# A decoder layer in one kernel: router counts spread over more passes, turned tiles in another bank, transposes and W1 products in another place

## The chip, the core and the metric

The kernel runs on one core of a Trainium2 chip. The metric is the device time of one execution in microseconds (us); lower is better. Before the change the median of three runs is 849.79 us (848.02 to 852.45). The profile is one further execution with its own time. Engines: PE is TensorE (matmuls; PEld its weight loads), DVE is VectorE, ACT is ScalarE, POOL is GpSimd, SP issues DMAs.

## What is computed

A decoder layer in float32 on x of 2 batches, 1024 tokens, 256 channels, with a context of 77 tokens for each batch:

```python
x = layernorm(x + causal_self_attention_with_rope(x))        # 16 heads of 64
x = layernorm(x + cross_attention(x, ctx))                   # 16 heads, 77 keys
weights = x @ w_r + b_r                                      # router: one number for each token
threshold = top_k(weights, 512)[-1]                          # per batch
selected = weights > threshold
block = gelu(x @ W1 + b1) @ W2 + b2                          # 256 -> 1024 -> 256
x = layernorm(x + where(selected, block, x))
```

## The kernel before

The tokens of both batches form 16 tiles of 128. The self-attention fills the first 584 us and is left alone by the change. Behind it comes `Prepare` (584 to 617 us): it folds the keys with the query weights (`wqk`) and the values with the output weights; the folded values are stored to DRAM by SP (`vo_d`, L727) and loaded back in another layout (`packed`, L728 and L729), per batch.

**Cross-attention, tile by tile.** `Tile_.turn` (L896) transposes the tile's x on TensorE into a bank of PSUM, and ACT copies it out as `x1T`. `scores` (L903) multiplies it with `wqk`; VectorE takes the maxima (L918) and subtracts them (L920), ACT takes exponentials, `weights` (L926) sums them on VectorE (L929, L931) and scales `e` on GpSimd (L932). `transposes` (L934) turns `e` in ten blocks on TensorE (L942), four to a bank, so in three groups with two blocks in the last; ACT copies them out as `pT`. `output` (L949) multiplies with `packed` (L954); VectorE adds x (y, L956) and starts the layer norm. Its `close` runs later: GpSimd's power (`rs`, L127), VectorE's scaling (x, L128) and the router's dot product (`weigh`, L761), which gives one number in `route`.

**The ring.** The banks that `turn`, `transposes`, `output`, `spread`, `slots`, and the feed-forward's `layer` write come from one pool of four (`ring`), handed out in the order in which the program asks. A bank may be written again when the engine that reads it has done so.

**The router.** A token is taken if fewer than 512 of its batch have a router value at least as large, so each tile's values are compared with all 1024. `spread(first, last)` (L765) transposes the values of tiles first to last so that every partition holds them in a row, and ACT copies the row to `every` (L772). `reach(i, first, last)` (L774) counts on VectorE, for the 128 tokens of tile i, how many values of tiles first to last reach theirs (L777). `select` (L783) makes a 0/1 mask and sums over tiles; `slots` (L789) sums over partitions with two matmuls (L792, L793) and gives each row a place; `scatter` (L805) writes each tile's rows to those places in DRAM with one indirect DMA of GpSimd for a tile (L807); `load` (L813) reads the two halves back as `kept[0]` (taken) and `kept[1]` (SP, L819) once all eight scatters have landed.

**Feed-forward.** `turn` (L838) transposes `kept[0]` (L843); `hidden(f0)` (L846) makes two of the eight W1 blocks, eight matmuls (L852), with gelu on ACT; `layer(j)` (L859) multiplies with W2 (L863), adds b2 (L868), puts x in where fewer than 512 were taken (L869), adds x (L870) and norms; `skipped(j)` (L882) handles the other half. GpSimd writes the rows out (L833).

**What sets the order.** From L978 on, TensorE, VectorE and ACT run in the order in which the program is written; the order on GpSimd and SP is left to the framework's scheduler. The loop (L1019) has passes s = 0 to 16. A pass holds, in this order: the scores and weights of tile s + 1, `output` of tile s - 1, what `midway` has for s, `turn` of tile s + 2, `transposes` of tile s, the `close` of tile s - 1, and what `at_end` has for s. So tile 7, the last of batch 0, is closed in pass 8. Batch 0's counts come in passes 7 to 10, its slots in 11, its scatters in 11 and 12, its load in 13; in pass 15 its rows are turned and batch 1's first six tiles are spread, and after that pass's `close` come `hidden(0)` of batch 0 and six counts of batch 1. Behind the loop come `hidden(2)`, the last two tiles' spread and counts of batch 1, `hidden(4)`, `hidden(6)`, batch 1's slots and scatters, W2 of batch 0 (`late`), batch 1's load and turning, and its feed-forward.

Of the kernel before, what the change touches and what calls it, by code (L numbers as in the profile page):

```python
# [34 lines left out]
def decoder_layer(  # L35
# [117 lines left out]
    with (  # L153
# [74 lines left out]
        class Pair:  # L228
# [151 lines left out]
            def output(self, n):  # L380
                if n == 0:
                    self.po = [ring.tile([P, NT, R32], F32, tag="t", name="po_self") for _ in range(4)]
                for k in range(4):
                    for j in range(2):
                        first = (NT * n + n, NT * (n + 1) + n)[j]
                        step = (1, NT)[j]
                        last = first + (NT - 1 - n) * step + 1

                        for r in range(k if n == NT - 1 else 0, 4):
                            rows = slice(r * R32, (r + 1) * R32)  # L390
                            TE.matmul(  # L391
                                self.po[r][j * D : (j + 1) * D, n:, :],
                                self.v4[rows, 4 * n + k, j * D : (j + 1) * D],
                                p_t[rows, first:last:step, k * R32 : (k + 1) * R32],
                                start=(n == 0 and k == 0), stop=(n == NT - 1 and k == r),
                            )
# [349 lines left out]
    class Router:  # L746
# [15 lines left out]
                dead, self.x2[:, i, :C], w_r, 1.0, b_r, ALU.mult, ALU.add, self.route[:, i : i + 1]  # L762
            )

        def spread(self, first, last):  # L765

            for m in range(first, last, 4):
                e = min(m + 4, last)
                pt = ring.tile([P, 4, P], F32, tag="t", name="pt_r")
                for i in range(m, e):  # L770
                    TE.transpose(pt[:, i - m, :], self.route[:, i : i + 1].to_broadcast([P, P]), ident)
                A.copy(self.every[:, m * P : e * P], pt[:, : e - m, :].rearrange("p i n -> p (i n)"))  # L772

        def reach(self, i, first, last):  # L774

# [37 lines left out]
        def load(self):  # L813
# [3 lines left out]
            for h in range(2):  # L817
# [5 lines left out]
                    tc.add_manual_dep(ins.ins, of.name, sync, reason="all rows are there")  # L823
                self.kept.append(t)

        def numbers(self):
            for t in self.kept:
                r = fp.tile([P, NK2], U32, tag="rows", name="rows", bufs=4)
                V.tensor_copy(r, t[:, :, C])
                self.rows.append(r)  # L830
# [28 lines left out]
        def layer(self, j):  # L859

            po = ring.tile([P, C], F32, tag="t", name="po_ffn")
            for f in range(NF):
                TE.matmul(  # L863
                    po, self.h_t[:, f, j * P : (j + 1) * P], w2[:, f, :], start=(f == 0), stop=(f == NF - 1)
                )
            x2 = self.kept[0][:, j, :C]
            y = fp.tile([P, C], F32, tag="yf", name="y", bufs=5)
            V.tensor_tensor(y, po, b2, ALU.add)  # L868
            V.copy_predicated(y, self.left[:, j : j + 1].to_broadcast([P, C]), x2)  # L869
            V.tensor_tensor(y, y, x2, ALU.add)  # L870
            return self.finish(0, j, y)

        def finish(self, h, j, y):
# [15 lines left out]
    class Tile_:  # L889
# [4 lines left out]
            self.x1 = x1s[b][:, i, :C]  # L894

        def turn(self):  # L896
            self.x_t = c2.tile([P, NC, P], F32, tag="x1T", name="x1T")
            pt = ring.tile([P, NC, P], F32, tag="t", name="pt_x")
            for c in range(NC):
                TE.transpose(pt[:, c, :], self.x1[:, c * P : (c + 1) * P], ident)  # L900
            A.copy(self.x_t, pt)  # L901
# [29 lines left out]
            V.reciprocal(inv, sums)  # L931
            G.tensor_tensor(e, e, inv.unsqueeze(2).to_broadcast([P, HH, S]), ALU.mult)  # L932

        def transposes(self):  # L934
            self.p_t = c2.tile([P, NK, P], F32, tag="pT2", name="pT2")
            e = self.e.rearrange("p h s -> p (h s)")
            for m in range(0, NK, 4):
                n = min(4, NK - m)
                pt = ring.tile([P, 4, P], F32, tag="t", name="pt_p2")
                for k in range(m, m + n):  # L940
                    w = min(P, HS - k * P)
                    TE.transpose(pt[:w, k - m, :], e[:, k * P : k * P + w], ident)  # L942
                whole = n if (m + n) * P <= HS else n - 1
                A.copy(self.p_t[:, m : m + whole, :], pt[:, :whole, :])
                if whole < n:
                    w = HS - (m + whole) * P
                    A.copy(self.p_t[:w, m + whole, :], pt[:w, whole, :])

        def output(self):  # L949

            po = ring.tile([P, C], F32, tag="t", name="po_cross")
            for k in range(NK):
                w = min(P, HS - k * P)
                TE.matmul(po, self.p_t[:w, k, :], packed[self.b][:w, k, :], start=(k == 0), stop=(k == NK - 1))  # L954
            y = work.tile([P, C], F32, tag="y", name="y", bufs=6)
            V.tensor_tensor(y, po, self.x1, ALU.add)  # L956
            last = layernorm(self.x1, y)

            def close():
                last()  # L960
                routers[self.b].weigh(self.i)

            return close

    tiles = [Tile_(b, i) for b in range(B) for i in range(NT)]
    L = NT - 2

    def reaches(r, tiles_, first, last):
        for i in tiles_:
            r.reach(i, first, last)  # L970

    def reached(r):

        reaches(r, range(L), L, NT)
        reaches(r, range(L, NT), 0, NT)
        r.select()

    with tc.manual_schedule(engines={TE.engine, V.engine, A.engine}):  # L978
        first = Prepare()
        k_t = first.context("k")  # L980
        first.turn()
        tiles[0].turn()
        tiles[1].turn()
        first.fold_keys(k_t)
        v_t = first.context("v")
        first.fold_values(v_t, 0)
        first.fold_values(v_t, 1, 0, NP // 2)
        for hh in range(2):
# [12 lines left out]
        wpool = pool("weights", 1)  # L1001
        w1 = load_wide(L0_ffn_W1, "wk")
        w2 = load_tall(L0_ffn_W2)
        routers = [Router(b) for b in range(B)]
        r0, r1 = routers


        midway = {
            L + 1: lambda: r0.spread(0, L), NT + 1: lambda: r0.spread(L, NT), NT + 3: r0.slots,
            NT + L + 1: lambda: (r0.turn(), r1.spread(0, L)),  # L1010
        }
        at_end = {
            NT - 1: lambda: reaches(r0, range(0, 3), 0, L), NT: lambda: reaches(r0, range(3, L), 0, L),
            NT + 1: lambda: reaches(r0, range(L), L, NT),
            NT + 2: lambda: (reaches(r0, range(L, NT), 0, NT), r0.select()),
            NT + 3: lambda: r0.scatter(0, 4), NT + 4: lambda: r0.scatter(4, NT), NT + 5: r0.load,
            NT + 6: r0.numbers, NT + 7: lambda: (r0.hidden(0), reaches(r1, range(L), 0, L)),
        }
        for s in range(B * NT + 1):  # L1019
            if 1 < s + 1 < B * NT:  # L1020
                for hh in range(2):
                    tiles[s + 1].scores(hh)
                for hh in range(2):
                    tiles[s + 1].weights(hh)
            close = tiles[s - 1].output() if s > 0 else None
            midway.get(s, lambda: None)()
            if s + 2 < B * NT:
                tiles[s + 2].turn()
            if s < B * NT:
                tiles[s].transposes()  # L1030
            if close:
                close()
            at_end.get(s, lambda: None)()

        r0.hidden(2)
        r1.spread(L, NT)
        reached(r1)
        r0.hidden(4)
        r0.hidden(6)
        r1.slots()  # L1040
        r1.scatter(0, NT)
        late = [r0.layer(j) for j in range(NK2)]
        r1.load()
        r1.turn()
        for f in late:
            f()
        for f in [r0.skipped(j) for j in range(NK2)]:
            f()
        r1.numbers()
        for f0 in range(0, NF, 2):  # L1050
            r1.hidden(f0)
        for f in [r1.skipped(j) for j in range(NK2)]:
            f()
        for j in range(NK2):
            r1.layer(j)()
# [39 lines left out]
```

## Time and profile before

| | us |
|---|---|
| median of three runs | 849.79 (848.02 to 852.45) |
| the profiled execution's own time | 851.71 |
| its span, first to last instruction | 849.9 |
| busy: TensorE, VectorE, ACT, GpSimd | 791.4, 572.0, 357.4, 364.1 |
| mean granted clock of TensorE | 0.982 of full |
| loop, first scores in it to its last output | 620.4 to 778.3 |
| batch 0's slot product | 729.30 |
| batch 0's scatters on GpSimd | 734.08 to 744.15 |
| batch 1's slot product | 789.70 |
| batch 1's scatters on GpSimd | 791.64 to 801.58 |
| last W2 product's end | 841.6 |

A row of the waits names who waited, for whom, and the total, the number and the longest of these waits. A timeline row gives start and length in us, engine, line, operation, output and inputs, and in brackets the idle time ahead of it with what ended it. A windows row gives, after the stretch and its length, busy time and number of instructions of PE, PEld, DVE, ACT and POOL, then the granted clock (1.00 is full speed), the DMA engines' mean busy share and GB/s. Times are read off one profiled execution.

### The profile page before, as it was taken

What the parts mean: (1) busy time and instruction counts of PE and PEld (TensorE: products, weight loads), DVE (VectorE), ACT (ScalarE), POOL (GpSimd) and SP (SyncE); (2) the same over time, 40 slices, a digit from 0 to 9 for tenths busy, and PEclk for the clock granted to TensorE, in tenths of its full rate; (3) what the DMA queues carried; (4) which work ended last, traced back from release to release, by engine and by line L of the source; (5) the groups of instructions that cost most, each with busy time, mean ns of one, the idle gap of its engine ahead of it and who ended that gap; (6) DMA issues with size and microseconds to landing.
All of it is one profiled execution on the core that took longest, in us unless ns stands there. A gap on an engine that the chain in (4) does not pass through costs nothing.

```text
span 849.9 us, 26576 instructions
## 1 busy us (share of the span) xinstructions
PE 791.4 (93%) x11428; PEld 627.2 (74%) x11428; DVE 572.0 (67%) x1306; ACT 357.4 (42%) x845; POOL 364.1 (43%) x261
## 2 busy tenths in 40 slices
PE   7979999999999999899999988789999999999886
PEld 4547788878778778678788776678778887776645
DVE  2566679767858757578668677444577788866654
ACT  2545556555555556365454554101433333223020
POOL 1732654563573564274372740212023322440473
PEclk9989999999999999999999999999999999999989
DMA  4564596596677669566485377572270000110130
GB/s 160 155 156 99 134 231 148 150 246 163 164 170 189 143 178 237 155 196 168 134 236 116 115 187 187 142 252 82 81 257 1 1 1 1 42 59 1 52 122 25
DMA packets 75040, 113.38 MB, mean 133 GB/s; under 512 B 7249, under 2 KB 61483, under 8 KB 72875
## 3 DMA queue, kind: packets, MB, share of 16 engines
q1 hardware_dynamic: 70315, 73.92, 29.0%
q10 hardware_dynamic: 3072, 33.56, 18.2%
q0 software_dynamic: 1536, 4.20, 1.3%
q8 instruction: 90, 1.47, 0.7%
q14 instruction: 27, 0.22, 0.1%
HBM read 71.77 MB, written 23.11 MB: 112 GB/s over the span
## 4 chain that ended last, share of the span: by engine, by line
PE 79%; DVE 10%; DMA 4%; issue 4%; POOL 2%; ACT 1%; SPq 0%; POOLq 0%; ACTq 0%; DVEq 0%
PE po_self L391 16%; PE ps_scores L323 16%; PE pp_kq L250 13%; PE pp_v L285 6%; PE ps_cross L911 6%; PE po_cross L954 6%; PE po_proj L452 5%; PE po_ffn L863 3%; PE pp_h L852 3%; DVE pT L353 2%; DVE reach L777 2%; DMA v_d<-v 1%; DVE p L336 1%; PE pt_p L942 1%; DVE e L920 1%
## 5 line engine op out<-in xcount | busy, mean ns | idle before, releaser
L344 ACT ACTIVATE p<-p,neg 128x768 f32<-128x768 f32 (+7 forms) x256 | 196.2, 768 | 172.9 <-DVE neg L336 168.9
L336 DVE CUSTOM_DVE_ANT_0 p<-ps_scores,fence 128x512 f32<-128x512 f32 (+7 forms) x256 | 179.4, 750 | 130.2 <-PE ps_scores L323 130.0
L353 DVE STREAM_TRANSPOSE pT<-p 128x768 f32<-128x768 f32 (+7 forms) x256 | 175.6, 740 | 4.7 <-PE po_self L391 3.4
L391 PE MATMUL po_self<-pT,v 32*64 32x256 f32 (+6 forms) x7808 | 160.4, 298 | 19.1 <-issue 14.8
L391 PEld LDWEIGHTS po_self<-pT,v 32*64 32x64 f32 x7808 | 137.5, 132 | 46.1 <-issue 33.8
L323 PE MATMUL ps_scores<-kq 64*128 64x256 f32 (+3 forms) x1064 | 153.2, 419 | 5.5 <-POOL kq L277 5.0
L323 PEld LDWEIGHTS ps_scores<-kq 64*128 64x128 f32 x1064 | 94.9, 190 | 49.3 <-issue 29.3
L270 POOL TENSOR_TENSOR kq<-raw,cos 128x1024 f32<-128x1024 f32 x31 | 73.2, 2362 | 130.6 <-ACT raw L258 130.6
L250 PE MATMUL pp_kq<-xT,w_pair 128*128 128x256 f32 (+2 forms) x528 | 121.8, 384 | 4.0 <-DVE inv L365 2.1
L250 PEld LDWEIGHTS pp_kq<-xT,w_pair 128*128 128x128 f32 x528 | 90.2, 192 | 27.9 <-issue 11.6
L273 POOL TENSOR_TENSOR turned<-turned,sin 128x1024 f32<-128x1024 f32 x31 | 73.2, 2361 | 56.5 <-DMA turned<-raw 50.2
L127 POOL TENSOR_TENSOR rs<-ve,neg_half 128x1 f32<-128x1 f32 x48 | 27.3, 575 | 154.2 <-DVE ve L125 151.1
L932 POOL TENSOR_TENSOR e<-e,inv 128x616 f32<-128x616 f32 x32 | 38.3, 1218 | 116.6 <-DVE inv L931 55.7
L277 POOL TENSOR_TENSOR kq<-kq,turned 128x1024 f32<-128x1024 f32 x31 | 73.5, 2372 | 1.4
L954 PE MATMUL po_cross<-packed,pT 128*128 128x256 f32 (+1 forms) x320 | 71.8, 379 | 0.1
L911 PE MATMUL ps_cross<-wqk,x1T 128*128 128x308 f32 x256 | 69.3, 424 | 1.4 <-ACT x1T L901 1.4
L954 PEld LDWEIGHTS po_cross<-packed,pT 128*128 128x128 f32 (+1 forms) x320 | 60.8, 190 | 10.2 <-issue 0.5
L285 PEld LDWEIGHTS pp_v<-w_pair,xT 128*128 128x128 f32 x512 | 61.1, 192 | 3.2 <-issue 1.5
L285 PE MATMUL pp_v<-w_pair,xT 128*128 128x128 f32 x512 | 62.2, 275 | 0.0
L911 PEld LDWEIGHTS ps_cross<-wqk,x1T 128*128 128x128 f32 x256 | 47.4, 190 | 17.9 <-ACT x1T L901 1.7
L452 PE MATMUL po_proj<-wo,attnT 128*128 128x256 f32 x240 | 56.5, 389 | 3.3 <-DMA attnT<-attn_d 3.3
L924 ACT ACTIVATE e<-e 128x616 f32<-128x616 f32 x32 | 22.9, 717 | 79.2 <-DVE e L920 79.2
(121 smaller groups left out, 795.6 us busy)
## 6 DMA issues: line engine op xcount, KB each, us to landing
v<-v_d ACTq DMA_DIRECT2D x64, 512.0 KB, 7.7
turned<-raw SPq DMA_DIRECT2D x64, 256.0 KB, 5.0
v_d<-v SPq DMA_DIRECT2D x64, 128.0 KB, 4.3
over<-inv_d SPq DMA_DIRECT2D x32, 256.0 KB, 4.2
attn_d<-out_pair SPq DMA_DIRECT2D x15, 512.0 KB, 8.6
attnT<-attn_d SPq DMA_DIRECT2D x8, 512.0 KB, 5.3
attnT<-attn_d SPq DMA_DIRECT2D x3, 896.0 KB, 5.1
vo_d<-vo SPq DMA_DIRECT2D x2, 1232.0 KB
```

The source lines that it names most:

```text
L250: TE.matmul(pp[:, cols], self.w[:, c, "kq".index(of), :], x_ts[self.b, n][:, c, cols], start=(c == 0), stop=(c == NC - 1),)
L270: E.tensor_tensor(self.kq[:, :, n * NB : (n + 1) * NB], self.raw[n], self.twice(cos, n), ALU.mult)
L277: E.tensor_tensor(dst, dst, self.turned[n], ALU.add)
L285: TE.matmul(pv[:, i, :], x_ts[self.b, 2 * n // NT][:, c, toks], self.w[:, c, 2, :], start=(c == 0), stop=(c == NC - 1),)
L323: TE.matmul(self.ps[j][:, cols], self.kq[rows, 1, t * P : (t + 1) * P], self.kq[rows, 0, cols.start - at : cols.stop - at], start=True, st ...
L336: V.tensor_tensor_reduce(p[:, span], self.ps[j][:, span], fence[:, T - (t + 1) * P :], -SCALE, -MASKED, ALU.add, ALU.min, neg[:, i : i + 1],)
L344: A.activation(p[:, span], p[:, span], AF.Exp, bias=neg[:, i : i + 1], scale=-1.0, accum_out=self.sums[:, j, t : t + 1],)
L353: V.transpose(p_t[:, first : first + t * step + 1 : step, :], self.p[g, j][:, span].rearrange("p (n k) -> p n k", k=P),)
L391: TE.matmul(self.po[r][j * D : (j + 1) * D, n:, :], self.v4[rows, 4 * n + k, j * D : (j + 1) * D], p_t[rows, first:last:step, k * R32 : (k ...
L452: TE.matmul(self.po, of, wo[:, c, :], start=(c == 0), stop=(c == NP - 1))
L911: TE.matmul(ps[:, g, : Q * S], self.x_t[:, c, :], wqk[:, c, self.b, h : h + Q, :].rearrange("p h s -> p (h s)"), start=(c == 0), stop=(c = ...
L954: TE.matmul(po, self.p_t[:w, k, :], packed[self.b][:w, k, :], start=(k == 0), stop=(k == NK - 1))
```

## The change

It does six things. (1) `turn` of tile 2 moves ahead of the loop, and `turn` of tile s + 3 is done inside `transposes` of tile s, in the two free quarters of its last bank; its copy by ACT comes after that bank's other copies, and `x1T` gets three buffers. (2) Batch 0's counts are split finer and begin in pass 5 with four tiles' values (passes 5 to 10), scatters are written two to a pass in passes 11 to 14, and batch 1's counts begin in pass 13. (3) The loop ends with pass 14; the last tile's transposes come ahead of the output of the tile before it, and batch 1's seventh value row is spread in the middle of the last output. (4) `hidden(0)` of batch 0 moves behind the last output, the last value row is copied by VectorE, and `hidden(4)` and `hidden(6)` come after batch 1's slots. (5) `ready` adds b2 to `kept[0]` and doubles `kept[0]` ahead of time, so that `layer` has one addition fewer. (6) In the built program the scheduler's order changes on SP: the loads of W1 and W2 (L95, L101) now stand ahead of vo's store and packed's load instead of behind them. The order on GpSimd is the same as before, with all eight scatters of a batch together.

The core of the diff:

```diff
-        def spread(self, first, last):
+        def spread(self, first, last, copy=A.copy):
...
+        def ready(self):
+            x2 = self.kept[0][:, :, :C]
+            self.plus = fp.tile([P, NK2, C], F32, tag="plus", name="plus")
+            V.tensor_tensor(self.plus, x2, b2.unsqueeze(1).to_broadcast([P, NK2, C]), ALU.add)
+            self.double = fp.tile([P, NK2, C], F32, tag="double", name="double")
+            V.tensor_tensor(self.double, x2, x2, ALU.add)
...
-            V.tensor_tensor(y, po, b2, ALU.add)
-            V.copy_predicated(y, self.left[:, j : j + 1].to_broadcast([P, C]), x2)
-            V.tensor_tensor(y, y, x2, ALU.add)
+            V.tensor_tensor(y, po, self.plus[:, j, :], ALU.add)
+            V.copy_predicated(y, self.left[:, j : j + 1].to_broadcast([P, C]), self.double[:, j, :])
...
-            self.x_t = c2.tile([P, NC, P], F32, tag="x1T", name="x1T")
+            self.x_t = c2.tile([P, NC, P], F32, tag="x1T", name="x1T", bufs=3)
...
-        def transposes(self):
+        def transposes(self, ahead=None):
...
+                if ahead and m + n == NK:
+                    ahead.x_t = c2.tile([P, NC, P], F32, tag="x1T", name="x1T", bufs=3)
+                    for c in range(NC):
+                        TE.transpose(pt[:, n + c, :], ahead.x1[:, c * P : (c + 1) * P], ident)
                 A.copy(self.p_t[:, m : m + whole, :], pt[:, :whole, :])
...
+                if ahead and m + n == NK:
+                    A.copy(ahead.x_t, pt[:, n : n + NC, :])
...
-        def output(self):
+        def output(self, midst=None):
...
+                if midst and k == NK // 2:
+                    midst()
...
+        tiles[2].turn()
...
-            L + 1: lambda: r0.spread(0, L), NT + 1: lambda: r0.spread(L, NT), NT + 3: r0.slots,
-            NT + L + 1: lambda: (r0.turn(), r1.spread(0, L)),
+            5: lambda: r0.spread(0, 4), 7: lambda: r0.spread(4, 6), 9: lambda: r0.spread(6, NT), 11: r0.slots,
+            13: lambda: r1.spread(0, 4), NT + 7: lambda: r1.spread(4, 6),
...
-            NT - 1: lambda: reaches(r0, range(0, 3), 0, L), NT: lambda: reaches(r0, range(3, L), 0, L),
-            NT + 1: lambda: reaches(r0, range(L), L, NT),
-            NT + 2: lambda: (reaches(r0, range(L, NT), 0, NT), r0.select()),
-            NT + 3: lambda: r0.scatter(0, 4), NT + 4: lambda: r0.scatter(4, NT), NT + 5: r0.load,
-            NT + 6: r0.numbers, NT + 7: lambda: (r0.hidden(0), reaches(r1, range(L), 0, L)),
+            5: lambda: reaches(r0, (0, 1), 0, 4), 6: lambda: reaches(r0, (2, 3), 0, 4),
+            7: lambda: reaches(r0, range(4), 4, 6), 8: lambda: reaches(r0, (4, 5), 0, 6),
+            9: lambda: reaches(r0, range(6), 6, NT), 10: lambda: (reaches(r0, (6, 7), 0, NT), r0.select()),
+            11: lambda: r0.scatter(0, 2), 12: lambda: r0.scatter(2, 4),
+            13: lambda: (r0.scatter(4, 6), reaches(r1, (0, 1), 0, 4)),
+            14: lambda: (r0.scatter(6, NT), reaches(r1, (2, 3), 0, 4)),
...
-        for s in range(B * NT + 1):
+        for s in range(B * NT - 1):
...
-            if s + 2 < B * NT:
-                tiles[s + 2].turn()
-            if s < B * NT:
-                tiles[s].transposes()
+            tiles[s].transposes(tiles[s + 3] if s + 3 < B * NT else None)
...
+        r0.load()
+        tiles[-1].transposes()
+        close = tiles[-2].output()
+        midway[NT + 7]()
+        r0.turn()
+        close()
+        reaches(r1, range(4), 4, 6)
+        reaches(r1, (4, 5), 0, 6)
+        close = tiles[-1].output(lambda: r1.spread(6, 7))
+        reaches(r1, range(6), 6, 7)
+        r1.reach(6, 0, 7)
+        close()
+        r0.hidden(0)
+        r1.spread(7, NT, V.tensor_copy)
+        reaches(r1, range(7), 7, NT)
+        r1.reach(7, 0, NT)
+        r1.select()
         r0.hidden(2)
-        r1.spread(L, NT)
-        reached(r1)
+        r1.slots()
+        r1.scatter(0, NT)
+        r0.numbers()
+        r0.ready()
         r0.hidden(4)
         r0.hidden(6)
-        r1.slots()
-        r1.scatter(0, NT)
         late = [r0.layer(j) for j in range(NK2)]
...
         r1.numbers()
+        r1.ready()
```

More of the change, by code (lines that the diff above doesn't have):

```diff
@@ L771, in spread @@
                     TE.transpose(pt[:, i - m, :], self.route[:, i : i + 1].to_broadcast([P, P]), ident)
-                A.copy(self.every[:, m * P : e * P], pt[:, : e - m, :].rearrange("p i n -> p (i n)"))
+                copy(self.every[:, m * P : e * P], pt[:, : e - m, :].rearrange("p i n -> p (i n)"))
         def reach(self, i, first, last):
@@ L865, in layer @@
                 )
-            x2 = self.kept[0][:, j, :C]
             y = fp.tile([P, C], F32, tag="yf", name="y", bufs=5)
-            V.tensor_tensor(y, po, b2, ALU.add)
-            V.copy_predicated(y, self.left[:, j : j + 1].to_broadcast([P, C]), x2)
-            V.tensor_tensor(y, y, x2, ALU.add)
+            V.tensor_tensor(y, po, self.plus[:, j, :], ALU.add)
+            V.copy_predicated(y, self.left[:, j : j + 1].to_broadcast([P, C]), self.double[:, j, :])
             return self.finish(0, j, y)
@@ L965, in decoder_layer @@
     tiles = [Tile_(b, i) for b in range(B) for i in range(NT)]
-    L = NT - 2
     def reaches(r, tiles_, first, last):
@@ L970, in reaches @@
             r.reach(i, first, last)
[L972 to L976, printed above, removed]
     with tc.manual_schedule(engines={TE.engine, V.engine, A.engine}):
@@ L1008, in decoder_layer @@
         midway = {
-            L + 1: lambda: r0.spread(0, L), NT + 1: lambda: r0.spread(L, NT), NT + 3: r0.slots,
-            NT + L + 1: lambda: (r0.turn(), r1.spread(0, L)),
+            5: lambda: r0.spread(0, 4), 7: lambda: r0.spread(4, 6), 9: lambda: r0.spread(6, NT), 11: r0.slots,
+            13: lambda: r1.spread(0, 4), NT + 7: lambda: r1.spread(4, 6),
         }
         at_end = {
-            NT - 1: lambda: reaches(r0, range(0, 3), 0, L), NT: lambda: reaches(r0, range(3, L), 0, L),
-            NT + 1: lambda: reaches(r0, range(L), L, NT),
-            NT + 2: lambda: (reaches(r0, range(L, NT), 0, NT), r0.select()),
-            NT + 3: lambda: r0.scatter(0, 4), NT + 4: lambda: r0.scatter(4, NT), NT + 5: r0.load,
-            NT + 6: r0.numbers, NT + 7: lambda: (r0.hidden(0), reaches(r1, range(L), 0, L)),
-        }
-        for s in range(B * NT + 1):
-            if 1 < s + 1 < B * NT:
+            5: lambda: reaches(r0, (0, 1), 0, 4), 6: lambda: reaches(r0, (2, 3), 0, 4),
[4 more added lines that the diff above has]
+            14: lambda: (r0.scatter(6, NT), reaches(r1, (2, 3), 0, 4)),
+        }
+        for s in range(B * NT - 1):
+            if s > 0:
                 for hh in range(2):
```

## Prediction

> **What bounds the kernel now.** I read the page first, then TensorE's waits in the part that the change can touch, then the timelines of TensorE, VectorE and GpSimd there. The built program of the changed kernel holds the same instructions in the same order up to 590 us, so only the last 260 us count.
>
> ```profile
> PE 791.4 (93%) x11428; PEld 627.2 (74%) x11428; DVE 572.0 (67%) x1306; ACT 357.4 (42%) x845; POOL 364.1 (43%) x261
> ...
> PE 79%; DVE 10%; DMA 4%; issue 4%; POOL 2%; ACT 1%; SPq 0%; POOLq 0%; ACTq 0%; DVEq 0%
> ```
>
> TensorE carries the end, and the edit removes no matmul. So it can only win TensorE's waits, and the half clock that follows a long one. Who waited for whom on TensorE, 615 to 850 us (total, times, longest):
>
> ```profile
> PE pt_x L843 <- DMA kept<-comp: 5.4, 1, 5.4
> PE pt_p L942 <- DVE y L956: 3.8, 4, 1.4
> PE ps_cross L911 <- ACT x1T L901: 1.4, 1, 1.4
> PE pp_slot L792 <- DVE sums L787: 0.7, 1, 0.7
> PE pp_h L852 <- ACT x2T L844: 0.5, 1, 0.5
> ```
>
> That is 11.8 us. TensorE's timeline shows where, and what the longest wait does to the work behind it:
>
> ```profile
> 729.92 0.60 PE L942 MATMUL pt_p<-ident,e 128*128 128x128 f32 x4
> 731.93 0.84 PE L942 MATMUL pt_p<-ident,e 128*128 128x128 f32 x6 [1.41 <-DVE y L956]
> ...
> 753.34 0.44 PE L942 MATMUL pt_p<-ident,e 128*128 128x128 f32 x2 [1.23 <-DVE y L956]
> ...
> 809.60 1.94 PE L843 MATMUL pt_x<-ident,kept 128*128 128x128 f32 x8 [5.40 <-DMA kept<-comp]
> 812.00 15.80 PE L852 MATMUL pp_h<-x2T,w_wk 128*128 128x512 f32 x32 [0.46 <-ACT x2T L844]
> ```
>
> The eight transposes of batch 0 take 0.95 (767.84 to 768.79); here 1.96. Thirty-two W1 products at 3.44 per eight (the first of batch 0) are 13.8; here 15.80. So 3.0 us are lost to a clock that the windows show at half:
>
> ```profile
> 804.00:808.00 4.00, 0.20 (x1) 0.00 (x0) 3.59 (x12) 0.00 (x0) 1.21 (x2) 1.00 0.25 53
> 808.00:816.00 8.00, 5.94 (x13) 3.32 (x14) 5.92 (x21) 1.49 (x4) 6.79 (x9) 0.57 0.49 156
> ```
>
> **Part 1, the start.** Tile 2's turning moves ahead of the loop. In pass 0 its transposes stand directly ahead of tile 2's scores, which wait for ACT's copy: 1.4. Afterwards the same two transposes (0.22) stand at 591 us and scores follow without that copy. The extra ACT copy (0.37) falls among copies that wait for VectorE there. **Minus 1.4.**
>
> SP's order changes as well: both FFN weights (1 MB each) now stand ahead of the store of vo and the load of packed. They wait for the last w_v product (601.5), so they do not hold SP (vo's store issues at 606.05), but they share the DMA engines with it. At some 380 GB/s (367, 420 and 347 in 628 to 634) their 2.1 MB take 5.5 us; started at 602.6 they leave 1.2 us of data when the store's first bytes move (606.9). packed lands at 619.4 now, 620.6 then; the first output needs it at 623.0. Cover 2.4, so I cost it at nothing. The other bound: the store waits until both have landed, 10.7 after their issue as now, and starts 6.5 later; that is rival 2.
>
> **Part 2, the loop.** A pass is 9.78 us of TensorE (640.10 to 649.88). A ring of four banks is allotted in order. A pass now takes five (output, turned tile, three of weights), so the third group of weights reuses the bank of its own output and waits for y. With the turned tile in the last bank a pass takes four, and the conflict is left only in passes with counts or slots: 5, 7, 9, 11, 13.
>
> How late is y? When VectorE is behind, it takes 8.07 from the first maximum to the end of the router's dot product (693.51 to 701.58; 1.03 of it waits for GpSimd's rs), y starts at 4.92, and TensorE resumes 0.52 after that start. When it keeps up, the dot product ends 11.49 after the pass's start (690.71 - 679.22). Counts come on top, by their spacing: 0.46 each at 256 wide, 0.934 at 768, 1.20 at 1024; I work out 0.67 at 512 and 1.07 at 896. 128 wide has no row: its columns alone are 0.13, the 256-wide row is 0.46; a line through it with the columns' slope gives 0.33, which I take. Lag of the first maximum behind the pass's start, worked forward (next lag = lag + 8.07 + counts - pass): for before it gives 3.77, 4.86, 4.7, 5.7 in passes 8 to 11, as the trace has it. Step lengths less work give before's true losses: 0.98 + 0.55 + 1.63 + 1.44 = 4.6.
>
> After: counts of 1.34, 1.34, 1.85, 1.87, 2.77, 3.2 (with the selection) in passes 5 to 10 instead of 2.8, 2.8, 2.8, 3.2 in 7 to 10. Lags 2.6, 3.1, 3.3, 3.6, 4.5, 5.9 in passes 6 to 11. In 5, 7 and 9 y is still on time (8.67), so no wait. In pass 11 y starts at 10.87, TensorE resumes at 11.39 and wanted 9.72: 1.7 lost, as before.
>
> Pass 13 hangs on GpSimd:
>
> ```profile
> 733.12 0.55 POOL L127 TENSOR_TENSOR rs<-ve,neg_half 128x1 f32<-128x1 f32 x1
> 734.08 1.20 POOL L807 DMA_INDIRECT comp<-x,slot  x1 [0.42 <-DVE slot L803]
> ...
> 743.19 0.96 POOL L807 DMA_INDIRECT comp<-x,slot  x1 [0.30 <-issue]
> 744.18 2.39 POOL L932 TENSOR_TENSOR e<-e,inv 128x616 f32<-128x616 f32 x2
> 746.53 0.57 POOL L127 TENSOR_TENSOR rs<-ve,neg_half 128x1 f32<-128x1 f32 x1
> ```
>
> Eight scatters (10.1 us) stand ahead of e and rs, and VectorE waits 4.6 for rs. The edit writes two scatters a pass, but GpSimd's queue is not ordered by hand: the built program still has all eight together ahead of tile 13's e. So this part does not do what it says. VectorE is again 5.9 late in pass 13, which now holds four counts' transposes: 1.5 lost. Loop: 4.6 becomes 3.2, **minus 1.4**. Were the scatters in written order, batch 0's rows would come in pass 15 instead of 13; they are not.
>
> **Part 3, the last transposes.** They now follow tile 14's at once. Their second half needs e from GpSimd, 6.67 after the first maximum, which lags 3.8 there: 10.5, wanted 10.0. **Plus 0.6**; a 0.2 wait between transposes and output goes. Batch 0's rows land near pass 13's middle, so their turning does not wait.
>
> **Part 4, behind the loop.** Here the end is set by batch 1's chain: last output, norm, counts, slots, eight scatters, load. From the slot product to the rows' landing it was 19.8 (789.70 to 809.47), the scatters 10.0 of it. Behind the slots stood only W2 (13.9): hence 5.4. Now hidden(4) and hidden(6) stand there too: 0.5 + 6.9 + 13.9 = 21.3, so the 5.4 and its 3.0 of half clock go, with 1.5 to spare.
>
> What is late next: more of the chain must now be crossed with less to do. From output 14's end VectorE has 0.2 + 1.27 (y to ve) + 0.6 (rs) + 0.95 (x, dot), four counts at 256 and two at 768 (3.7), y of tile 15 (1.27), then, queued ahead of x of tile 15, six counts at 128 and one at 896 (3.1), x and dot 0.95: 12.0. TensorE has count transposes and turning 1.35, output 15 with one more 4.43, hidden(0) 3.44: 9.2. It stops 2.8 to 2.9 at spread(7). After that: copy on VectorE 0.5, seven at 128 and one at 1024 (3.6), selection 0.8 = 4.9 against hidden(2) 3.55: 1.4 to 1.5 more.
>
> Does a gap of 2.9 throttle? The row first: after this stop the windows of half a microsecond show the clock at 0.50 from 515.5 to 518.5.
>
> ```profile
> 514.47 1.47 PE L391 MATMUL po_self<-pT,v 32*64 32x128 f32 x73 [2.53 <-issue]
> ```
>
> The Trainium skill (TensorE: Matmul & The Clock Gate, "Part 1: The HAM clock gate") has the clock halved only after a whole idle window of about 3.4 us; by it 2.9 costs nothing. By the row it costs 1.7 (3.4 us at half), but on hidden(2), which ends ahead of the 1.5 wait for slots and is covered by it. I take the row, 0.3 uncovered; bounds 0 and 1.7.
>
> The sums plus and double (two of 128x1024, by 799 ns for 616 wide some 1.3 each) fall on VectorE while TensorE runs hidden(4): nothing; without that cover 2.6. At the end one 0.45 addition after the last W2 product goes: **minus 0.45**. Tail: 0.9 + 5.4 + 3.0 = 9.3 becomes 2.9 + 1.5 + 0.3 + 0.1 = 4.8, **minus 4.5**.
>
> **Sum.** -1.4 -1.4 +0.6 -0.2 -4.5 -0.45 = -7.35. The profiled execution took 851.71 (span 849.9 and 1.8 around it), 1.9 above the median of 849.79: it goes to 844.4, the median to 842.4.
>
> **Rivals.** (1) Narrow counts cost what 256 does (thirteen of them, +0.13 each: 1.7) and the half clock after the gap is uncovered (1.7): 845.8. For it: 256 wide is already above its slope. (2) Weights ahead of vo: packed 6.5 later, the first output stops 2.9, half clock 1.7: 847.0. Against it: the DMA engines stood idle from 600 to 606, so the weights have a start. (3) Slower: the gap at spread(7) starts a half clock that does not end, because hidden(2) and the slots' wait keep TensorE idle by turns. It costs half of the time it lasts; it decides from 23.3 us at half on, which the 24.7 us of work up to batch 0's last W2 product could fill; at 25 us it gives 854.9. Against it: the longest stretch here is 6.8 (808.8 to 815.7). (4) Better: passes 11 and 13 lose nothing: 839.2.
>
> **Chances.** Forecast (840 to 845) 0.62; (4) 0.12; (1) 0.14; (2) 0.08; (3) 0.04. A measurement tells 0.5% (4.2 us) from no change: faster 0.74, same 0.22, slower 0.04. Range 838.5 to 847: (4) without its lower edge, (1) and (2).
>
> **What would show it.** No wait of pt_x for kept in batch 1, and W1 at 13.8 there; a new stop of nearly 3 us at the last count's transpose and one near 1.5 at the slots; in the loop, waits of pt_p for y in passes 11 and 13 alone; eight scatters together. I am wrong if batch 1's rows still come late (slots over 1.5 us later), if VectorE's lag at tile 15 is larger, or if the first output waits for packed.

## The result and the profile after

| | before | after |
|---|---|---|
| median of seven runs (us) | 851.85 (848.02 to 855.7) | 844.62 (843.15 to 849.51) |
| profiled execution: its own time | 851.71 | 849.51 |
| its span | 849.9 | 847.7 |
| from Prepare's first product to batch 0's slot product | 145.02 | 142.07 |
| to batch 1's slot product | 205.42 | 199.53 |
| to the turning of batch 1's rows | 225.32 | 220.73 |
| to the end of the last W2 product | 257.34 | 250.28 |
| to the end of the span | 265.62 | 261.25 |
| end of the span after the last W2 product | 8.28 | 10.97 |

The ratio is 0.994, 95% interval 0.991 to 0.9969. A second measurement on another chip gave 0.9939 (0.9901 to 0.9977). The forecast was 842.4 of 849.79, which is 0.9913: the right side, but by these ratios only two thirds of the gain came. The ratio is not the quotient of the medians. These are 7.2 apart on both chips (851.15 and 843.9 on the other), as much as forecast, but the runs behind each of them spread over 6 to 11, so their agreement with the forecast proves nothing.

The six lower rows are the sharp measure. The self-attention ahead of Prepare is the same code in all kernels, and yet it took between 578.4 and 588.4 in the profiles of this study; this spread is most of what makes the times vary by 1 to 2% (the spans of two profiles of the changed kernel differ by 2.7, their self-attention by 3.0). From Prepare's first product on, two profiles of the changed kernel agree within 0.3 (261.25 and 261.51). By this measure the change is worth 4.4 and 4.1 instead of 7.35. Up to the last W2 product it is worth 7.1 and 7.2 (6.9 forecast), and 2.7 to 3.1 are lost behind it. One caution: there is one profile of the kernel before, and W1 behind the stop for kept took 15.80 in it; behind the same stop it took 14.96 and 14.98 in two other kernels ("no ready" and "turned tile alone" below). So some 0.8 of these gains is how long the half clock happened to last.

TensorE's waits in the part from 610 us on, of the changed kernel, in the order of the prediction's list:

```profile
PE pt_r L771 <- DVE route L761: 2.8, 1, 2.8
PE pt_p L949 <- DVE y L971: 2.6, 2, 1.3
PE pp_h L860 <- ACT x2T L852: 0.6, 1, 0.6
PE pt_p L949 <- POOL e L938: 0.3, 1, 0.3
PE pp_slot L792 <- DVE sums L787: 0.2, 1, 0.2
```

Gone are the waits for kept (5.4) and x1T (1.4); y makes TensorE wait twice instead of four times; new is the stop of 2.8 at the last spread. The sum is 6.5 instead of 11.8. TensorE's timeline in the tail:

```profile
780.63 0.45 PE L771 MATMUL pt_r<-ident,route 128*128 128x128 f32 x1 [2.79 <-DVE route L761]
780.87 4.88 PE L860 MATMUL pp_h<-x2T,w_wk 128*128 128x512 f32 x8
785.98 0.36 PE L792 MATMUL pp_slot<-sums,ones 128*128 128x9 f32 x2 [0.23 <-DVE sums L787]
...
807.18 1.12 PE L851 MATMUL pt_x<-ident,kept 128*128 128x128 f32 x8
808.91 14.00 PE L860 MATMUL pp_h<-x2T,w_wk 128*128 128x512 f32 x32 [0.61 <-ACT x2T L852]
```

The turning of batch 1's rows waits for nothing, and its W1 runs at full clock (14.00 instead of 15.80). But TensorE no longer sets the end. The chain that ended last, from 816 us (start, length, what):

```profile
816.11 0.44 DVE y L892
816.56 3.67 DMA kept<-comp
820.29 0.29 DVE rows L837
820.58 1.01 DVE plus L830
821.59 1.13 DVE double L832
822.72 0.35 DVE y L892
...
830.50 3.40 issue
...
839.92 0.43 DVE y L875
```

In words: the last read of batch 0's skipped rows (y, 816.11) frees the only buffer of kept[1]; batch 1's second half is loaded into it; then come rows, plus and double, and batch 1's four skipped rows. GpSimd's timeline shows what the 3.40 called "issue" was:

```profile
828.43 1.04 POOL L841 DMA_INDIRECT out_dram<-y,rows  x1 [0.18 <-issue]
...
832.30 0.96 POOL L841 DMA_INDIRECT out_dram<-y,rows  x1 [0.30 <-issue]
833.29 0.57 POOL L127 TENSOR_TENSOR rs<-ve,neg_half 128x1 f32<-128x1 f32 x1
```

The first layer's rs stands behind the four writes of skipped rows. The layers then go at the pace of VectorE and GpSimd, 2.85 each, and the last y starts at 839.92, 3.2 after the last W2 product (836.73). In the kernel before, the skipped rows were done at 823.1 and layer 0's y came at 831.3, so this chain had 8 us of slack. The chain that ended last did not show it there; the idle time of VectorE did:

```profile
831.29 0.42 DVE L868 TENSOR_TENSOR y<-po_ffn,b 128x256 f32<-128x256 f32 x1 [8.16 <-PE po_ffn L863]
```

### The profile page after: what moved, and what is told of

It reads as the page before. It is cut to its first block, busy times and chain, and to the rows that moved or that the text cites. A ratio compares the mean times of both kernels' runs of the same rounds, so it can differ in the third digit from the quotient of the medians.

```text
span 847.7 us, 26624 instructions
## 1 busy us (share of the span) xinstructions
PE 787.5 (93%) x11428; PEld 626.5 (74%) x11428; DVE 576.2 (68%) x1333; ACT 356.6 (42%) x845; POOL 365.7 (43%) x261
## 3 DMA queue, kind: packets, MB, share of 16 engines
q8 instruction: 90, 1.47, 0.7%
## 4 chain that ended last, share of the span: by engine, by line
PE 74%; DVE 11%; DMA 5%; issue 5%; POOL 3%; ACT 1%; SPq 0%; POOLq 0%; ACTq 0%; DVEq 0%
PE po_self L391 16%; PE ps_scores L323 15%; PE pp_kq L250 12%; PE ps_cross L917 6%; PE pp_v L285 6%; PE po_cross L969 6%; PE po_proj L452 5%; DVE pT L353 2%; DVE reach L777 2%; PE po_ffn L871 2%; DMA v_d<-v 2%; DVE p L336 1%; PE pt_p L949 1%; DMA turned<-raw 1%; DMA attnT<-attn_d 1%
## 5 line engine op out<-in xcount | busy, mean ns | idle before, releaser
L323 PE MATMUL ps_scores<-kq 64*128 64x256 f32 (+3 forms) x1064 | 150.0, 413 | 6.4 <-POOL kq L277 5.9
L452 PEld LDWEIGHTS po_proj<-wo,attnT 128*128 128x128 f32 x240 | 46.1, 195 | 10.8 <-issue 4.2
```

Of the source, the lines that this page charges most:

```text
L323: TE.matmul(self.ps[j][:, cols], self.kq[rows, 1, t * P : (t + 1) * P], self.kq[rows, 0, cols.start - at : cols.stop - at], start=True, st ...
L452: TE.matmul(self.po, of, wo[:, c, :], start=(c == 0), stop=(c == NP - 1))
```

## The experiments

In the expectations, "end" is the stretch from the last W2 product to the end of the span. All ratios are to the kernel before on the same chip; "stage" is from Prepare's first product to the end of the span.

| kernel | ratio (95% interval) | stage | batch 1's slots | its rows' turning | last W2's end | end |
|---|---|---|---|---|---|---|
| before | 1 | 265.62 | 205.42 | 225.32 | 257.34 | 8.28 |
| after | 0.994 (0.991 to 0.9969) | 261.25 | 199.53 | 220.73 | 250.28 | 10.97 |
| after, again | 0.9939 (0.9901 to 0.9977) | 261.51 | 199.35 | 220.55 | 250.10 | 11.41 |
| ready behind | 0.9956 (0.9932 to 0.9981) | 260.32 | 199.49 | 220.62 | 250.16 | 10.16 |
| kept[1] twice | 0.9951 (0.9929 to 0.9974) | 260.70 | 199.38 | 220.58 | 250.13 | 10.57 |
| both | 0.994 (0.9909 to 0.9972) | 259.61 | 199.41 | 220.61 | 250.16 | 9.45 |
| turned tile alone | 0.9965 (0.9944 to 0.9987) | 261.69 | 202.31 | 222.20 | 253.40 | 8.29 |
| W1 first | 0.9963 (0.9941 to 0.9984) | 264.54 | 205.97 | 224.23 | 256.63 | 7.91 |
| scatters in order | 1.0004 (0.9982 to 1.0026) | 265.43 | 203.47 | 224.68 | 254.22 | 11.21 |
| no ready | 1.0013 (0.9995 to 1.0031) | 265.65 | 199.37 | 226.14 | 257.32 | 8.33 |
| tail, close first | 0.992 (0.9891 to 0.9949) | 257.95 | 199.56 | 218.83 | 250.10 | 7.85 |
| early skipped rows | 0.9914 (0.989 to 0.9939) | 257.94 | 199.38 | 220.59 | 250.13 | 7.81 |
| three cures | 0.9859 (0.9826 to 0.9893) | 254.63 | 197.55 | 217.30 | 246.87 | 7.76 |
| three cures, ready early | 0.986 (0.9839 to 0.9882) | 253.54 | 197.70 | 216.16 | 245.73 | 7.81 |

**What sets the end.** Three edits of the changed kernel, each at another link of the chain. First, `ready` behind the skipped rows:

```diff
         r1.numbers()
-        r1.ready()
...
         for f in [r1.skipped(j) for j in range(NK2)]:
             f()
+        r1.ready()
```

> The changed kernel with batch 1's plus and double moved behind the norm of its skipped rows. Theory (the end hangs on VectorE and GpSimd: kept[1] lands, plus and double, skipped rows, their four writes, then rs of layer 0): the skipped rows start 2.2 us earlier (two sums at 1.22 a piece, spaced 1.1), so do their writes (828.4 becomes 826.2), rs of layer 0 and the last y: end after the last W2 product 11.1 becomes 8.9, time 844.6 becomes 842.4. Rival (the end is set by GpSimd's own pace or by the landing of writes, whatever stands ahead of them): 0, 844.6.

Then a second buffer for kept[1], and both edits together:

```diff
-                t = f1.tile([P, NK2, C + 1], F32, tag=f"kept{h}", name="kept")
+                t = f1.tile([P, NK2, C + 1], F32, tag=f"kept{h}", name="kept", bufs=1 + h)
```

> The changed kernel with two buffers for kept[1], so that batch 1's second load need not wait for the last read of batch 0's skipped rows. Theory: kept[1] lands near 808 instead of 820, VectorE's 1.52 of waiting for it goes, the skipped rows start 1.5 earlier, time 844.6 becomes 843.1. Rival (GpSimd's pace): 0. If the load that now moves beside other traffic makes kept[0] later, the turning of kept[0] stops, and the time rises.

> Both edits together: the skipped rows start 3.75 earlier, at 818.9; then TensorE sets the last y again (its own lateness behind the last W2 product was 3.3): minus 3.3, 841.3, and the end 7.8 after the last W2 product (8.27 before, one addition of 0.45 fewer). Rival: 844.6, end still 11 after it.

Each moved the stage in the forecast direction and by half of the forecast: against the mean of the two profiles of the changed kernel (261.4) by 1.1, 0.7 and 1.8 instead of 2.2, 1.5 and 3.3. The ratios can't tell effects of this size. The missing half is on GpSimd; its timeline in the first of the three:

```profile
819.95 1.04 POOL L841 DMA_INDIRECT out_dram<-y,rows  x1 [0.18 <-issue]
821.30 2.15 POOL L841 DMA_INDIRECT out_dram<-y,rows  x1 [0.30 <-issue]
823.75 0.96 POOL L841 DMA_INDIRECT out_dram<-y,rows  x1 [0.30 <-DVE y L876]
```

Plus and double run from 820.25 to 822.6 on VectorE there, and the write beside them takes 2.15 instead of 0.96. In these three kernels GpSimd paid 1.2 to 1.7 for them (2.62 with the second buffer, 2.14 with both); in the changed kernel they stood beside writes of batch 0, off this chain, and cost GpSimd 0.8 (two writes of 1.51 and 1.17). So both sides of the expectation had something: the chain is what sets the end, and GpSimd's pace takes part of each cure away.

The next edit takes the chain away at its head. Batch 0's skipped rows are there since pass 14, so they are computed behind batch 0's `ready`, while VectorE waits for W2:

```diff
         r0.ready()
+        skips = [r0.skipped(j) for j in range(NK2)]
...
-        for f in [r0.skipped(j) for j in range(NK2)]:
+        for f in skips:
             f()
```

In `skipped`, y gets buffers of its own (tag `ys`): in the changed kernel the y at 816.11 waits 0.86 for a write to free one of the five that it shares with `layer`. The run does not separate the two parts of this edit.

> The first cure alone: batch 0's skipped rows ahead of its W2, with y buffers of their own. Theory: kept[1] of batch 1 comes without a wait, TensorE sets the end again, 7.8 after the last W2 product instead of 11.0 to 11.4: 261.4 - 3.4 = 258.0. Rival (GpSimd's twelve writes set it): the end stays 10 to 11 after it, 261.

The end is 7.81 after the last W2 product, and the last y again waits for TensorE:

```profile
831.42 0.42 DVE L875 TENSOR_TENSOR y<-po_ffn,plus 128x256 f32<-128x256 f32 x1 [0.57 <-PE po_ffn L871]
```

The stage is 3.4 shorter, as expected. With that the place of the loss is shown. The addition saved in `layer` shows as well once TensorE sets the end: 7.81 against 8.28 in the kernel before.

**What made the wait for kept, and what took it away.** First the W1 products put back ahead of the slots, with all else as changed (`r0.hidden(4)` and `r0.hidden(6)` ahead of `r1.slots()`):

> The changed kernel with the third and fourth W1 pairs of batch 0 ahead of batch 1's slots again, as before. Theory (the tail is batch 1's chain, and what lies behind the slots must cover its 20 us): slot product 6.3 later, rows 6.3 later, TensorE stops some 5 for kept and its W1 runs 3 longer at half clock; the end gets its slack back (3.3 less after the last W2 product): 844.6 + 5.0 + 3.0 - 3.3 = 849.3. Rival (the finer counts alone made the tail shorter, the place of the W1 products is worth nothing): 844.6.

The slot product is 6.5 later, TensorE stops 3.84 for kept (not 5), and W1 behind it takes 16.19, part of it at half clock:

```profile
812.59 1.93 PE L851 MATMUL pt_x<-ident,kept 128*128 128x128 f32 x8 [3.84 <-DMA kept<-comp]
814.98 16.19 PE L860 MATMUL pp_h<-x2T,w_wk 128*128 128x512 f32 x32 [0.46 <-ACT x2T L852]
```

That is 3.1 of stage, of 4.7 expected. Then part 5 undone (`ready` gone, `layer` as before):

> The changed kernel with part 5 undone: no plus and double, three steps in each layer as before. Measured from the first product behind the self-attention to the end of the span (265.6 in the kernel before, 261.3 and 261.5 in two profiles of the changed one). Theory: the two sums stand on the chain of the end, so without them the skipped rows and their writes start 2.2 earlier; the layers then go at 3.3 instead of 2.85 each and the last norm is 0.46 longer: 260.4, so part 5 cost 0.9 where I had booked a gain of 0.45. GpSimd's first scatter of batch 1 and its writes, which took 1.5 to 2.6 beside the two sums, take 0.96 to 1.1 again. Prediction's view (part 5 is worth 0.45, its sums nothing): 261.8.

This was the surprise. I expected a small gain and got a loss of 4.3: the kernel is no faster than the one before. The end has its slack back (8.33), as the theory says, and the first scatter takes 1.06, but TensorE's timeline has the old stop, although the slots are where they were:

```profile
807.09 1.94 PE L851 MATMUL pt_x<-ident,kept 128*128 128x128 f32 x8 [5.40 <-DMA kept<-comp]
809.49 14.96 PE L860 MATMUL pp_h<-x2T,w_wk 128*128 128x512 f32 x32 [0.46 <-ACT x2T L852]
```

SP's own waits there name who held the load, after the scatters had landed:

```profile
SPq L819 <- DVE y L878: 8.5, 1, 8.5
```

L878 is the last addition of `layer`, which reads kept[0] of batch 0. There is one buffer for kept[0], and without `ready` its last reader is the last layer behind all of W2; `ready` moves that reader ahead of W2. SP's waits and the chain of the kernel before, read again, have the same:

```profile
SPq L819 <- DVE y L870: 1.6, 1, 1.6
```

```profile
805.17 0.44 DVE y L870
805.61 0.02 SPq L819
805.63 0.04 issue
805.67 3.79 DMA kept<-comp
```

So the 5.40 of the kernel before was 3.8 of scatters and loading and 1.6 of waiting for the buffer. The two runs fit to a tenth: with `ready` and W1 ahead of the slots 3.84 is left; with W1 behind the slots and without `ready` the full 5.40. Only the two together take the stop away.

**The parts in the loop.** The turned tile in the last bank, alone, in the kernel before (with `tiles[2].turn()` ahead of the loop and three buffers of `x1T`):

> The kernel before with the turned tile in the weights' last bank and tile 2's turning ahead of the loop, nothing else. Theory: the wait for x1T at 621 goes (1.4); passes 10 and 13 no longer ask for a fifth bank, so their losses (0.55 and 1.44) go, and passes 9 and 11 (with spread and slots) keep 0.9 and 1.6: minus 3.4, 851.85 becomes 848.4. Rival (the loop's waits come from VectorE's lag and need the finer counts): minus 1.4 only, 850.4.

The ratio is 0.9965; the two waits for y left are 2.5 together, as worked out. The stop for kept is as before:

```profile
808.71 1.94 PE L843 MATMUL pt_x<-ident,kept 128*128 128x128 f32 x8 [5.39 <-DMA kept<-comp]
811.11 14.98 PE L852 MATMUL pp_h<-x2T,w_wk 128*128 128x512 f32 x32 [0.46 <-ACT x2T L844]
```

The stage is 3.9 shorter, but only 3.1 of it (3.4 expected) is there when batch 1's rows are turned; the other 0.8 is W1, 14.98 instead of 15.80 after the same stop, which is the clock and not this edit. Even so, this one edit gains the greater part of what the whole change does (4.4 and 4.1, with the same 0.8 in them).

The scatters as the program writes them: each pair from the second on also waits for the router's product of its pass (`r1.mark`, the instruction of `weigh`):

```diff
+                if behind:
+                    tc.add_manual_dep(ins.ins, behind.ins.name, sync, reason="in a later pass")
...
-            11: lambda: r0.scatter(0, 2), 12: lambda: r0.scatter(2, 4),
+            11: lambda: r0.scatter(0, 2), 12: lambda: r0.scatter(2, 4, r1.mark),
```

and so on for the pairs of passes 13 and 14.

> The changed kernel with its scatters of batch 0 really two to a pass: each later pair also waits for the router's dot product of its pass, which keeps GpSimd's queue in the written order. Theory: VectorE's 4.8 of waiting for rs in pass 12 goes, and with it pass 13's loss (1.3) and the 0.3 for e; but the last pair is issued near 763 to 766, its rows are read back near 772, and the turning of batch 0's rows, which stands at 767, stops about 5; 0.9 of this comes back at the last spread, 1 to 3 are lost to the half clock: 844.6 - 1.6 + 5.1 - 0.9 + 2 = 849. Rival (the change as it is written was better than as it was built): minus 1.6, 843.0.

Pass 13's wait for y and the one for e are gone, and TensorE stops in front of batch 0's rows:

```profile
765.83 1.94 PE L853 MATMUL pt_x<-ident,kept 128*128 128x128 f32 x8 [5.53 <-DMA kept<-comp]
```

The stage is 4.0 longer, the ratio 1.0004 against 0.9939 on the same chip. The order as built, all eight together, was the better one.

**The changed kernel again, and a better one.**

> The changed kernel itself, for a comparison on one chip with the next three and with the kernel before: ratio 0.994. In the two profiles of the first experiments with the same stop of 2.78 at the last spread the clock stayed full, in two (the changed kernel's and one other) it went to half; so here the stop should be 2.8 again and either the slots wait 1.5 at full clock or 0.2 at half, the slot product at the same distance from the stop.

The stop was 2.78, the clock stayed full, the slots waited 1.47. Then the tail alone:

```diff
         close = tiles[-1].output(lambda: r1.spread(6, 7))
+        close()
         reaches(r1, range(6), 6, 7)
         r1.reach(6, 0, 7)
-        close()
...
         r0.hidden(2)
+        r0.hidden(4)
         r1.slots()
...
-        r0.hidden(4)
         r0.hidden(6)
```

> The second cure alone: norm and dot product of the last tile ahead of the seven counts, one W1 pair more ahead of the slots. First product behind the self-attention to the end. Theory: stops of 2.8 and 0.2 to 1.5 become about 1.0, 1.8 come back for kept, so the last W2 product ends 1.5 earlier; but batch 0's layers end 3.3 earlier, and with them the chain that sets the end (skipped rows, kept[1], skipped rows of batch 1): 261.4 - 3.3 = 258.1, the end 9.3 after the last W2 product. Rival (TensorE sets the end): minus 1.5, 259.9.

The stops are 0.51 and 0.49, together the 1.0 worked out. The sum came as expected (257.95 against 258.1), its parts did not. The last W2 product comes no earlier (250.10, not 1.5 less), because kept takes back 1.34 and W1 runs 1.7 longer, with the clock at half from 805 to 808; all the same the stage is 3.5 shorter, since kept[1] of batch 1, with it the chain of the end, comes some 3.5 earlier, and the end follows 7.85 after that product instead of 9.3. Had TensorE set the end (the rival), an unmoved last W2 product would have left the stage as it was.

Both cures together, with scatters of three, three and two in passes 11 to 13 held in order by the same dependence (here the load of W2's weights stands behind packed again; TensorE waits for neither):

> The changed kernel with three cures. (1) Batch 0's skipped rows are computed right behind its plus and double, with y buffers of their own, so that batch 1's second load and its skipped rows come early: the end's 3.3 go. (2) The norm of the last tile and its dot product stand ahead of the seven counts, and one more W1 pair ahead of the slots, so that TensorE has 10.6 of work for the 11.6 that VectorE needs from the last output to the slots: the stops of 2.8 and 0.2 to 1.5 shrink to about 1 at the slots, and some 1.4 come back for kept: minus 2.1. (3) The scatters of batch 0 go three, three and two to passes 11 to 13, so that their rows still come in time: pass 13's 1.6 go. Theory: 844.6 - 3.3 - 2.1 - 1.6 = 837.6, end near 7.8 after the last W2 product. Rival (the end is set by GpSimd's writes): 841.

And with batch 0's `numbers` and `ready` moved behind `r0.load()`, ahead of the last tile's transposes:

> The kernel with three cures (254.63 from the first product behind the self-attention to the end, 838.1 in all), with plus and double of batch 0 moved into pass 14, where VectorE waits 2.3 for TensorE, instead of beside the scatters of batch 1. Theory (a sum of two operands of 1024 columns on VectorE holds up GpSimd's writing of descriptors: the first scatter took 1.92 there and 1.06 in the kernel before): the first scatter takes about 1.06, the rows of batch 1 come 0.9 earlier, the stop for kept goes from 1.8 to 0.9: 253.7. Rival (the first scatter of a group is slow for another reason): 254.6, first scatter 1.92.

Against the changed kernel the three cures bring 6.8 (7.0 expected), the fourth 1.1 more (0.9 expected). The first scatter of batch 1 on GpSimd with three cures:

```profile
785.06 1.92 POOL L807 DMA_INDIRECT comp<-x,slot  x1 [10.72 <-DVE slot L803]
```

and with `ready` early:

```profile
784.90 1.06 POOL L807 DMA_INDIRECT comp<-x,slot  x1 [10.72 <-DVE slot L803]
```

TensorE's stop for kept goes from 1.81 to 0.53. (The waits name VectorE for both; but the loads landed at 802.73 and 801.29, and TensorE went on 0.14 and 0.13 later, as it did 0.14 after the landing in the kernel before.) These two beat both kernels: on one chip, three cures took 838.1 where the changed kernel had 843.9 and the one before 851.15. Between the two the ratios can't decide, the stage (253.54 against 254.63) can.

## Why the prediction was right or wrong

**The start (minus 1.4) and the loop (minus 1.4): right.** Up to batch 0's slot product I had 1.4 + 0.98 + 0.55 = 2.93; it was 2.95. The wait for x1T is gone. The two waits for y left are 1.34 in pass 11 and 1.26 in pass 13 (1.7 and 1.5 worked out). A count of 128 columns is spaced 0.325 (0.33 taken from a line through wider ones), so the first half of rival 1 has no ground. packed's load issues 8.1 behind vo's store instead of 7.1, and the first output does not wait for it: rival 2 has none either. The last transposes lost 0.34 for e, not 0.6.

**That the scatters stay together: right**, and what the written order would do was half seen. I had said that the rows would come in pass 15; I had not said that this is dear. It costs 4.0.

**The gaps in the tail: right.** The stop at the last spread is 2.79 (2.8 to 2.9), the one at the slots 1.46 to 1.47 where the clock stayed full (1.4 to 1.5), and in this profile the half clock covers the latter (0.23 left):

```profile
781.00:782.00 1.00, 1.00 (x3) 0.48 (x2) 0.85 (x4) 0.00 (x0) 0.00 (x0) 0.50 0.03 8
783.00:784.00 1.00, 1.00 (x3) 0.33 (x2) 1.00 (x7) 0.00 (x0) 0.00 (x0) 0.78 0.00 0
```

So the row was a better guide than the rule of the Trainium skill (TensorE: Matmul & The Clock Gate, "Part 1: The HAM clock gate"), by which a stop under some 3.4 costs nothing. Eight profiles of this study have the same stop of 2.78 or 2.79: half clock followed in three (this one, `ready` behind, W1 first), not in five. So neither rule nor row holds alone. What I booked, nearly nothing, was right in all of them with the slots close behind, since the slot product waits for VectorE and comes at the same time (199.35 to 199.53); in the kernel with W1 first there is no such cover, and 24 products took 11.73, at 3.5 per eight without it 10.5. That is what rival 1 had called uncovered. Rival 3 (a half clock that doesn't end) did not come.

**Minus 4.5 for the tail: the size right, its cause in part wrong.** From batch 0's slot product to the last W2 product 4.1 were gained; minus 4.5 of the tail, plus 0.6 and minus 0.2 of part 3 make the same 4.1. The step that failed reads "From the slot product to the rows' landing it was 19.8 ... Behind the slots stood only W2 (13.9): hence 5.4." Of these 19.8 the last 1.6 ahead of the load were the wait for kept[0]'s buffer, held by the last layer's addition. I took a load that starts late for a chain that is long, because the wait on TensorE names only the load. With W1 behind the slots and no `ready` the stop stayed 5.40, so placing W1 there brings nothing by itself; that it worked is due to `ready`, which I had booked as an addition fewer. The size was right by luck. With `ready` the rows land 19.1 behind the slot product (781.28 to 800.40 in the kernel with two buffers for kept[1], whose tail is the same up to there): 1.6 less for the buffer and 0.9 more for the first scatter.

**Minus 0.45 for the end, and nothing for plus and double: wrong.** This is where the gain stayed: 2.7 to 3.1 more instead of 0.45 fewer. I costed `ready` for batch 0, where TensorE's W1 hides it, and not for batch 1, where it stands between the landing of kept[1] and the skipped rows. And I took the last W2 product for the end without asking how much slack the skipped rows had once TensorE came earlier: 8 us before, against 7 by which the last W2 comes earlier, 1 by which batch 0's W2 now ends later, and 2.2 for `ready`. What is late next must be asked of the chain at the end as well, not only of the stop that goes. That plus and double also hold up GpSimd was in no term of the sum; batch 0's two sums are the 0.9 of batch 1's first scatter.

## What to carry to other kernels

A tile with one buffer ties the next load to the last reader of the last use; ask the load's own queue what it waited for before you call a late load a long chain. An edit that looks like one addition fewer can be worth most because it moves that last reader, and its own cost can show in another batch, where nothing hides it. When TensorE is made earlier by some microseconds, work out the slack of every chain that ends beside it, down to the last write.

## What the runs showed of the hardware

**Sums on VectorE hold up GpSimd's indirect DMAs.** A scatter or write that began while plus or double ran (two operands in SBUF, 1024 columns, 1.22 each) took 1.48 to 2.75 in all these kernels; all others took 0.96 to 1.20, most of them 0.96. Batch 1's first scatter took 1.90 or 1.92 beside them, and 1.06 where they stood elsewhere or were gone (the kernel before, W1 first, no `ready`, `ready` early). The Trainium skill (SBUF — State Buffer, "Who interferes with whom") says that such a sum contends only with GpSimd's reads and infers that the writing of descriptors goes on. The places of an indirect DMA lie in a tile in SBUF here (`slot`, `rows`), so the reading of them may be the reason; no run here tells the two apart, nor whether two operands or the length of the sums matters.

**The half clock is not set by the length of the stop alone.** After a stop of 2.78 or 2.79 it came in three of eight profiles. After stops of 1.34 and 0.69, with only eight transposes between, it came in one kernel (tail, close first: 0.50 from 805 to 808):

```profile
802.88 1.06 PE L851 MATMUL pt_x<-ident,kept 128*128 128x128 f32 x8 [1.34 <-DMA kept<-comp]
804.64 15.70 PE L860 MATMUL pp_h<-x2T,w_wk 128*128 128x512 f32 x32 [0.69 <-ACT x2T L852]
```

After longer ones, 1.81 and 0.69 about the same eight transposes, it did not come in another (three cures):

```profile
802.87 1.06 PE L853 MATMUL pt_x<-ident,kept 128*128 128x128 f32 x8 [1.81 <-DVE ve L125]
804.62 14.00 PE L862 MATMUL pp_h<-x2T,w_wk 128*128 128x512 f32 x32 [0.69 <-ACT x2T L854]
```

What decides it stays open.
